# A two-layer GraphSAGE kernel on one core: nine dense groups instead of eight in layer 2, with h kept as two float32 parts for float32r products

## The chip, the core and the metric

The kernel runs on one core of one Trainium2 chip. The core has TensorE (PE) with its weight loads (PEld), VectorE (DVE), ScalarE (ACT), GpSimd (POOL) and the sync engine (SP), which here only issues transfers. The metric is the device time of one execution in microseconds, lower is better; of several executions the median is taken.

## The reference, cut to what matters

The inputs are x (12500 nodes x 256 features, float32), 200000 edges `src`, `dst` sorted by `dst`, and the weights of two layers and an output product. Low-numbered nodes have many more edges than high ones: `dst` is drawn as 12500 u^2.

```python
def _sage_conv(x, src, dst, W_l, b_l, W_r):
    msgs = x[src]
    agg = jax.ops.segment_sum(msgs, dst, num_segments=N_NODES)
    deg = jax.ops.segment_sum(jnp.ones((src.shape[0],), x.dtype), dst, num_segments=N_NODES)
    mean = agg / jnp.maximum(deg, 1.0)[:, None]
    return mean @ W_l + b_l + x @ W_r

h = relu(_sage_conv(x, src, dst, W1_l, b1, W1_r))
h = relu(_sage_conv(h, src, dst, W2_l, b2, W2_r))
out = layernorm(x + h @ W3 + b3)
```

## The kernel before

**Two ways to sum the edges.** Nodes are cut into 98 blocks of 128 (`NB = 98`), edges into 1563 tiles of 128. The destinations with the most edges are handled densely, in groups of 256 nodes (`DN = 256`). For such a group the kernel makes a table of counts (how often each of the 12544 source nodes points to each of the 256 destinations) in SBUF as bfloat16 and multiplies: the sums of the group are x^T times the counts, summed over all 98 source blocks. Layer 1 handles `HG1 = 6` groups (1536 nodes) in this way, layer 2 `HG = 8` groups (2048 nodes). All other edges are gathered: POOL issues one indirect transfer per tile (`L273`), which fetches 128 rows of 1 KB from x or h in DRAM. Four of them make a round. In a round four small products on PE (the strips, `part_ps`, L285) add up the rows of equal destination, ACT copies the result out (L295), a second product (`sum_ps`, L301) spreads it, and DVE adds it into a ring of sums (L315).

**Rounds set the order.** `layer` walks the rounds of gathers. Four buffers `got` hold the rows, so that POOL can be at most four rounds ahead of the strips on PE. PE and POOL run in the order in which the program is written; the other engines run their own queues in order too. After each round's strip the program places other work: pieces of the node blocks (the dense products with the weights), counting, and dense passes. How much goes into a round is set by a planner: each piece yields a cost for PE, DVE and ACT (`COST_1`, `COST_2` and so on), and a round is filled until the largest of the three loads reaches an allowance, 5.3 us in layer 1 and 5.2 us in layer 2. In the last rounds (8 in layer 1, 14 in layer 2) all that remains is placed.

**Layer 1's dense passes.** `count` makes the tables of the groups in the order 5, 4, 3, 2, 1, 0; two tables fit into SBUF (`both`), so each is used while the next one is made. `product` multiplies x with one table. Products of three bfloat16 parts of x give float32 accuracy; the parts lie in DRAM (`x3_d`) and are loaded for two blocks at a time (L747), six 256-column products per block (L750). As the parts do not exist at the start, the first pass and half of the second multiply float32 x with a widened float32 table (`wide`, L762, on ACT; L765 on PE), and these two passes make the parts on the side, one half of the blocks each (`parts`, L694 to L697: two DVE operations and two ACT copies per block). The tables of groups 5, 4, 3 and 2 are stored to DRAM for layer 2 (`stored`, seven transfers each).

**Layer 2's dense passes.** `first_block` writes h to DRAM, and its three bfloat16 parts to `h3_d`, again by `parts`. `products` takes two groups at a time: per block six products of 512 columns (L790), half of them into each of two PSUM tiles. Its rows are loaded for two blocks at a time (L717), four buffers deep. The first pass takes the tables of groups 1 and 0, which are still in SBUF; then come (5,4) and (3,2), whose tables are streamed from DRAM (L722) while the tables of 6 and 7 are counted, then (6,7) alone. Each finished group goes through `last_block`. A load of rows waits, by `freed`, for the strip that follows the last use of its buffer.

Of the kernel before, what the change touches and what calls it, by code (L numbers as in the profile page):

```python
# [8 lines left out]
F32 = mybir.dt.float32  # L9
# [16 lines left out]
P = 128  # L26
# [23 lines left out]
def by_runs(  # L50
# [55 lines left out]
    HG1, HG, DN = 6, 8, 256  # L106
# [6 lines left out]
    ROOMS = [5, 5, 7, 7] + [5] * 5 + [7] * 5 + [9] * 5 + [10] * 2  # L113
# [485 lines left out]
    SPLIT = 3  # L599
    split3 = keep.tile([P, SPLIT, 3, D], BF16, name="split")  # L600
# [10 lines left out]
    picks = [keep.tile([P, WIDEST * NB], BF16, name=f"pick{i}") for i in range(4)]  # L611
# [77 lines left out]
    def parts(t, s, rest):  # L689

        def upper(a):
# [8 lines left out]
    STREAMS = 4  # L700
    used_tables = tables[:, :sum(widths[:2 * HG1])]
    streams = [t.bitcast(BF16)[:, i * 4 * DN:(i + 1) * 4 * DN].rearrange("p (b g d) -> p b g d", b=2, g=2)
               for t in (spare, used_tables) for i in range(STREAMS // 2)]
# [9 lines left out]
    def loaded(b, pair):  # L713

        nonlocal n_streamed
        rows = rows_pool.tile([P, 2, 3, D], BF16, name="rows", bufs=N1)
        freed(nc.sync.dma_start(rows, h3_d[:, b:b + 2]), N1)  # L717
        counted = both[:, b:b + 2, :, :DN]
        if pair is not None:
            counted = streams[n_streamed % STREAMS]  # L720
            n_streamed += 1
            freed(nc.sync.dma_start(counted, count_d[:, b:b + 2, pair:pair + 2]), STREAMS)  # L722
        return rows, counted

    def product(g, c_sb, plain=range(0), made=range(0)):
# [4 lines left out]
        own, wide = {}, {}  # L730

        def x_rows(u):
            t = rows_pool.tile([P, 2, 3, D], BF16, name="rows", bufs=N1)
            t = t.rearrange("p b k d -> p (b k d)").bitcast(F32)[:, :2 * D].rearrange("p (b d) -> p b d", d=D)
            n = min(2, (N - u * P) // P)
            freed(nc.sync.dma_start(t[:, :n], x[u * P:(u + n) * P].rearrange("(b p) f -> p b f", p=P)), 1)
            if n < 2:
                left = N - (u + n) * P
                nc.vector.memset(t[:, n], 0.0)
                nc.sync.dma_start(t[:left, n], x[(u + n) * P:N])  # L740
            return t

        for b in range(NB):
            if b not in plain:
# [9 lines left out]
            else:  # L754
                if b % 2 == 0:
                    for u in range(b, min(b + 2 * N1 - 2, plain[-1]), 2):
                        if u not in own:
                            own[u] = x_rows(u)
# [749 lines left out]
```

## Time and profile before

| what | value |
|---|---|
| median of 3 runs | 2687.47 us (2685.69 to 2693.3) |
| profiled execution | 2681.34 us |
| its span | 2679.5 us |
| first to last gather of layer 1 | 11.4 to 1425.8 us, 1028 gathers |
| first to last gather of layer 2 | 1453.6 to 2637.0 us, 940 gathers |
| after the last gather | 42.5 us |
| granted clock of TensorE, mean | 0.968 |

The profile is of one execution. Busy times of PE overlap, since products are pipelined: the time that one product takes in a row of many is the distance from start to start, not its busy time. In the rows of a window a bracket like `(x940)` is the number of instructions. A wait is written as the engine and line that waits, then what ended the wait. Names of buffers have their numbers cut off, so `x_d` is `x3_d`, and `h_d` stands for both h and its parts.

### The profile page before, as it was taken

The numbers are of one execution on the slowest core, as the hardware profiler recorded it, in microseconds if no ns is written. First come the engines' busy times: TensorE is split into PE (matmuls) and PEld (weight loads), VectorE is DVE, ScalarE is ACT, GpSimd is POOL, SyncE is SP. The second block draws the span as 40 slices with busy tenths as digits, with TensorE's granted clock in tenths as the row PEclk, the third lists the DMA queues.
The fourth block names the chain that finished last, engine by engine and source line by source line (L and its number), as shares of the span: only waits on it lengthen the run. The fifth ranks groups of instructions, "written<-read, shape, count | busy, mean of one in ns | idle before, by whom it ended". The sixth has DMA issues, their size and how long they took to land. (4 is left out here: it accounts for less than half of the span.)

```text
span 2679.5 us, 51726 instructions
## 1 busy us (share of the span) xinstructions
PE 2411.8 (90%) x17119; PEld 1506.1 (56%) x17119; DVE 1558.3 (58%) x5514; ACT 1201.1 (45%) x2409; POOL 1910.2 (71%) x1978
## 2 busy tenths in 40 slices
PE   3678999889999999999997999999999999899986
PEld 2245676556776766666674445545455555555555
DVE  6777654775667789987334123544455554544455
ACT  0587764875667752386223012343434443222223
POOL 6767776776777777776664777777777777777772
PEclk8699999989999999999998999999999999999999
DMA  5359779889898777775875777778777777677653
GB/s 136 106 167 310 240 223 304 257 256 298 261 300 277 242 221 217 221 210 169 266 241 170 224 224 230 241 244 251 237 226 242 250 236 218 195 206 212 201 172 95
DMA packets 360737, 602.57 MB, mean 225 GB/s; under 512 B 56093, under 2 KB 244239, under 8 KB 360463
## 3 DMA queue, kind: packets, MB, share of 16 engines
q1 hardware_dynamic: 261637, 340.29, 39.8%
q0 software_dynamic: 94464, 258.08, 32.2%
q8 instruction: 141, 2.31, 0.4%
q10 hardware_dynamic: 4362, 0.80, 0.2%
q14 instruction: 133, 1.09, 0.1%
HBM read 509.09 MB, written 89.87 MB: 224 GB/s over the span
## 5 line engine op out<-in xcount | busy, mean ns | idle before, releaser
L273 POOL DMA_INDIRECT got<-in_x_dram,src_t x1028 | 1010.6, 983 | 412.3 <-issue 256.1
L273 POOL DMA_INDIRECT got<-h_d,src_t x940 | 897.3, 955 | 313.9 <-issue 251.4
L865 ACT CAST counts<-count_ps 128x882 f32 (+3 forms) x688 | 620.4, 902 | 232.7 <-PE count_ps L859 185.0
L859 PE MATMUL count_ps<-pick,low 128*128 128x490 bf16 (+2 forms) x1188 | 350.8, 350 | 56.9 <-ACT counts L865 44.9
L750 PE MATMUL dense_ps<-counts,rows 128*128 128x256 bf16 x2640 | 359.3, 276 | 23.3 <-DMA rows<-x_d 22.5
L285 PE MATMUL part_ps<-got,one 128*32 128x257 f32 (+1 forms) x3936 | 325.3, 403 | 58.7 <-DMA got<-h_d,src_t 34.8
L790 PEld LDWEIGHTS <-rows 128*128 128x128 bf16 x2352 | 214.0, 97 | 259.4 <-issue 81.4
L821 DVE TENSOR_SCALAR pick<-steps,tables 128x686 bf16<-128x686 f16 (+3 forms) x816 | 335.1, 411 | 24.7 <-PE count_ps L863 11.7
L295 ACT COPY some<-part_ps 128x257 f32<-128x257 f32 (+1 forms) x349 | 130.0, 373 | 472.5 <-PE part_ps L285 467.4
L750 PEld LDWEIGHTS <-rows 128*128 128x128 bf16 x2640 | 241.7, 98 | 104.8 <-issue 33.2
L229 DVE TENSOR_TENSOR one<-lo_t,lane_b 128x128 f32<-128x128 bf16 x492 | 140.7, 287 | 233.5 <-PE part_ps L285 232.3
L824 DVE TENSOR_SCALAR low<-lanes,low_t 128x130 bf16<-128x130 f16 x816 | 220.8, 272 | 82.5 <-PE count_ps L863 78.3
L315 DVE TENSOR_TENSOR sums<-sums,sum_ps 128x256 f32 x349 | 143.0, 410 | 154.6 <-PE sum_ps L301 134.8
L301 PE MATMUL sum_ps<-two,some 128*128 128x128 f32 x1396 | 222.6, 283 | 9.7 <-ACT own_t L997 7.6
L301 PEld LDWEIGHTS sum_ps<-two,some 128*128 128x128 f32 x1396 | 202.7, 195 | 41.4 <-ACT own_t L997 12.9
L790 PE MATMUL beside_ps<-counts,rows 128*128 128x512 bf16 x588 | 224.5, 382 | 0.5 <-ACT split L800 0.5
L790 PE MATMUL dense_ps<-counts,rows 128*128 128x512 bf16 x588 | 224.6, 382 | 0.0
L1038 DVE TENSOR_TENSOR own<-block_ps,biases 128x256 f32<-128x256 f32 x196 | 83.0, 424 | 216.9 <-PE block_ps L1031 214.5
L859 PEld LDWEIGHTS <-low 128*128 128x128 bf16 x1188 | 114.7, 99 | 150.4 <-issue 38.2
L285 PEld LDWEIGHTS part_ps<-got,one 128*32 128x32 f32 x3936 | 80.2, 109 | 202.5 <-issue 162.0
L997 ACT COPY own_t<-block_ps 128x256 f32<-128x256 f32 x294 | 105.4, 373 | 168.0 <-PE block_ps L995 164.8
L1034 ACT COPY sums<-zero 128x256 f32<-128x256 f32 x168 | 67.7, 403 | 240.9 <-PE block_ps L1031 240.9
(197 smaller groups left out, 3588.2 us busy)
## 6 DMA issues: line engine op xcount, KB each, us to landing
rows<-x_d SPq DMA_DIRECT2D x220, 384.0 KB
rows<-h_d SPq DMA_DIRECT2D x196, 384.0 KB
count_d<-counts SPq DMA_DIRECT2D x28, 896.0 KB
x_sb<-in_x_dram SPq DMA_DIRECT2D x194, 128.0 KB
h_d<-split SPq DMA_DIRECT2D x98, 192.0 KB
x_d<-split SPq DMA_DIRECT2D x98, 192.0 KB
rows<-in_x_dram SPq DMA_DIRECT2D x72, 256.0 KB
got<-in_x_dram,src_t POOLq DMA_INDIRECT x1028
```

The lines of the kernel that those rows point to most:

```text
L229: nc.vector.tensor_tensor(one, lo[:, a:a + n * (G - 1) + 1:n].unsqueeze(2).to_broadcast([P, G, W]), lane_b[:, :W].unsqueeze(1).to_broadcas ...
L273: rows = nc.gpsimd.indirect_dma_start(out=g[:, j, :D], out_offset=None, in_=self.table, in_offset=bass.IndirectOffsetOnAxis(ap=src_t[:, e: ...
L285: strip = nc.tensor.matmul(part_ps[j * W:(j + 1) * W, :width], lhsT=one[:, j], rhs=g[:, j, :width], start=r == 0, stop=r == n - 1)
L295: nc.scalar.copy(some[:, :width], part_ps[:, :width])
L301: nc.tensor.matmul(sum_ps[:, c], lhsT=some[:, c * P:(c + 1) * P], rhs=two, start=True, stop=True)
L315: adds.append(nc.vector.tensor_add(own, own, sum_ps[:, :NC]).ins)
L750: nc.tensor.matmul(ps[:, c], lhsT=rows[:, b % 2, k, c * P:(c + 1) * P], rhs=c_sb[:, b, :DN], start=False, stop=b == NB - 1 and k == 2 and ...
L790: nc.tensor.matmul(ps[c], lhsT=rows[:, b % 2, k, c * P:(c + 1) * P], rhs=counted[:, b % 2], start=b + k == 0, stop=b == NB - 1 and k == 2)
L821: nc.vector.tensor_scalar(r[:, :w * NB], steps[:, :w * NB], key_t[g][:, t - lo_g:t - lo_g + 1], None, op0=OP.is_equal)
L824: nc.vector.tensor_scalar(low.rearrange("p (a b) -> p a b", a=5), lanes_5[:, :, :LW // 5], low_t[:, t:t + 1], None, op0=OP.is_equal)
L859: nc.tensor.matmul(c[:, a * NB:b * NB], lhsT=s, rhs=r[:, a * NB:b * NB], start=True, stop=alone)
L865: nc.scalar.copy(to[:, :, bass.ds(off_act.at(t), w)], c.rearrange("p (d s) -> p s d", s=NB))
```

## The change

Layer 2:

- `HG` is 9: the destinations 2048 to 2303 become a dense group, and their edges are no longer gathered in layer 2.
- h is stored as two float32 parts (`exact`: the upper part by masking the low 12 bits of the float32, the lower as the difference), 2 KB per node instead of 1.5 KB. Both operations are on DVE; `parts` had two on DVE and two on ACT.
- The products take float32r operands. Per block and pair of groups there are four products of 512 columns instead of six. The bfloat16 tables must be widened to float32 first (`widened`, one ACT copy of 128x512 per block and pair).
- Rows are loaded per block (256 KB) into six buffers, issued four to five blocks ahead; tables are streamed per block into six buffers.
- The passes are (1,0), (5,4) while 6 and 7 are counted, (6,7), (3,2) while 8 is counted, and 8 alone. The last one has 256-column products, four per block, and one widening per two blocks.

Layer 1:

- No pass multiplies float32. The first pass makes the three bfloat16 parts of two blocks at a time (`parts_of`), writes them to `x3_d`, and multiplies them from the same buffer. All six passes have six 256-column bfloat16 products per block.

The allowances become 5.05 us in layer 1 and 5.04 us in layer 2. `pick` has three buffers instead of four, `split` two instead of three. `sums_a`, `sums_b` and `w3_sb` lie in parts of other tiles that are no longer needed.

```diff
-    HG1, HG, DN = 6, 8, 256
+    HG1, HG, DN = 6, 9, 256
-    h3_d = dram.tile([P, NB, 3, D], BF16, name="h3_d")
+    h2_d = dram.tile([P, NB, 2, D], F32, name="h2_d")
-    SAVED = ORDER[:HG1 - 2] + ORDER[HG1:HG - 2]
+    SAVED = ORDER[:HG1 - 2]
-    SPLIT = 3
-    split3 = keep.tile([P, SPLIT, 3, D], BF16, name="split")
+    split = keep.tile([P, 2, 2, D], F32, name="split")
-    picks = [keep.tile([P, WIDEST * NB], BF16, name=f"pick{i}") for i in range(4)]
+    picks = [keep.tile([P, WIDEST * NB], BF16, name=f"pick{i}") for i in range(3)]
+    def exact(t, s):
+        nc.vector.tensor_scalar(s[:, 0].bitcast(I32), t.bitcast(I32), -4096, None, op0=OP.bitwise_and)
+        nc.vector.tensor_tensor(s[:, 1], t, s[:, 0], op=OP.subtract)
-    STREAMS = 4
+    STREAMS = 6
+    N2, WIDE = 6, 4
-    def loaded(b, pair):
+    def loaded(b, of, back):
-        rows = rows_pool.tile([P, 2, 3, D], BF16, name="rows", bufs=N1)
-        freed(nc.sync.dma_start(rows, h3_d[:, b:b + 2]), N1)
+        rows = rows_pool.tile([P, 2, D], F32, name="rows", bufs=N2)
+        freed(nc.sync.dma_start(rows, h2_d[:, b]), back)
...
+    def widened(counted):
+        wide = rows_pool.tile([P, 2, DN], F32, name="wide", bufs=WIDE)
+        nc.scalar.copy(wide.bitcast(F32R), counted)
+        return wide
+    def parts_of(t, s):
+        rest = rows_pool.tile([P, 2, D], F32, name="rest_2", bufs=1)
+        nc.vector.tensor_tensor(rest, t, upper(t), op=OP.subtract)
+        freed(nc.vector.tensor_tensor(s[:, :, 2], rest, upper(rest), op=OP.subtract), N1)
+        freed(nc.scalar.copy(s[:, :, 0], upper(t)), N1)
+        nc.scalar.copy(s[:, :, 1], upper(rest))
...
-    def products(gs, pair):
+    def products(gs):
+        for b in range(0, NB, 2):
+            for u in range(b, min(b + 6, NB)):
+                if u not in held:
+                    held[u] = loaded(u, gs, b - (u - N2))
+            for u in range(b, min(b + 4, NB)):
+                if u not in wide:
+                    wide[u] = wide[u - 1] if one and u % 2 else widened(held[u][1])
...
+                            nc.tensor.matmul(ps[c], lhsT=own[:, k, c * P:(c + 1) * P].bitcast(F32R),
+                                             rhs=of.bitcast(F32R), start=u + k == 0,
+                                             stop=u == NB - 1 and k == 1)
...
-    COST_FIRST, COST_1, COST_2 = (0.92, 0.0, 0.31), (0.68, 0.0, 0.0), (0.7, 0.0, 0.0)
-    COST_DEGREES, COST_SPLIT, COST_REST = (0.4, 0.0, 0.0), (0.0, 0.71, 0.81), (0.0, 0.0, 0.3)
+    COST_ONE = 1.1, 0.0, 0.65
+    COST_FIRST, COST_1, COST_2 = (0.68, 0.61, 0.7), (0.68, 0.0, 0.0), (2.0, 0.0, 1.24)
+    COST_DEGREES, COST_REST = (0.4, 0.0, 0.0), (0.0, 0.0, 0.3)
...
+        yield [passed(*ORDER[4:6])]
+        yield [passed(*SAVED[0:2]), (next_counts(ORDER[6:8]), counting(*ORDER[6:8]))]
+        yield [passed(*ORDER[6:8])]
+        yield [passed(*SAVED[2:4]), (next_counts(ORDER[8:]), counting(*ORDER[8:]))]
+        yield [passed(*ORDER[8:])]
...
-        layer(gathers_1, first_block, 3, staged(stages_1), 5.3, 8)
+        layer(gathers_1, first_block, 3, staged(stages_1), 5.05, 8)
...
-    layer(Gathers(h_d, True), last_block, 5, staged(stages_2), 5.2, 14)
+    layer(Gathers(h_d, True), last_block, 5, staged(stages_2), 5.04, 14)
```

`COST_2` was the cost of three products and is now that of two blocks, which have eight; `COST_ONE` and `COST_FIRST` are for two blocks of the pass of group 8 and for one block of layer 1's first pass.

More of the change, by code (lines that the diff above doesn't have):

```diff
@@ L1075, in first_block @@
         nc.sync.dma_start(h_d[b * P:(b + 1) * P, :], h)
[L1076 to L1079 removed]
+        s = split[:, b % 2]
+        exact(h, s)
+        nc.sync.dma_start(h2_d[:, b], s)
+        yield 1.75, 1.65, 1.1
     def last_block(b, agg=None):
```

160 lines of the change are left out of this document (67 added, 93 removed).

## The prediction

> **What bounds the kernel now.** First the page's head and a table of stretches: up to the last gather of layer 1, between the layers, layer 2's gathers, the end.
>
> ```profile
> span 2679.5 us, 51726 instructions
> ...
> core 0: us, PE busy (x) PEld busy (x) DVE busy (x) ACT busy (x) POOL busy (x), PEclk, DMA share, GB/s
> 11.40:1425.80 1414.40, 1264.25 (x10145) 857.88 (x10145) 983.15 (x3664) 816.81 (x1571) 1010.62 (x1028) 0.95 0.75 235
> 1425.80:1453.60 27.80, 16.24 (x86) 11.21 (x84) 14.83 (x49) 11.15 (x32) 0.01 (x1) 0.91 0.52 171
> 1453.60:2637.00 1183.40, 1103.90 (x6752) 616.72 (x6752) 530.57 (x1690) 360.78 (x772) 897.29 (x940) 0.99 0.72 221
> 2637.00:2679.50 42.50, 25.32 (x132) 18.57 (x130) 21.88 (x64) 12.39 (x35) 0.02 (x1) 0.94 0.20 57
> ```
>
> With the 11.4 us before the first gather: 11.4 + 1414.4 + 27.8 + 1183.4 + 42.5 = 2679.5. PE is the engine with the largest busy time, but that is modelled and overlaps; the question is what paces the rounds. Two neighbouring gathers, and the gathers by form:
>
> ```profile
> 2603.32 0.95 POOL L273 DMA_INDIRECT got<-h_d,src_t  x1 [0.30 <-issue]
> 2604.57 0.95 POOL L273 DMA_INDIRECT got<-h_d,src_t  x1 [0.30 <-issue]
> ```
> ```profile
> L273 POOL DMA_INDIRECT got<-in_x_dram,src_t x1028 | 1010.6, 983 | 412.3 <-issue 256.1 <-PE part_ps L285 119.0 <-DMA got<-in_x_dram,src_t 10.9
> L273 POOL DMA_INDIRECT got<-h_d,src_t x940 | 897.3, 955 | 313.9 <-issue 251.4 <-DMA h_d<-split 27.8 <-DMA got<-h_d,src_t 12.2
> ```
>
> A gather comes every 1.25 us when POOL waits for nothing: 0.95 busy, 0.30 between. Four make a round, so 5.0 us is the floor of a round. Layer 2 takes 1183.4/940 = 1.259 us for each, 8 us above its floor of 1175 in all; no wait for PE is in its row. **Layer 2 is paced by POOL.** Layer 1 takes 1414.4, 129 above its floor of 1028 x 1.25 = 1285, and its row names PE's strips (119.0 us): PE reaches them late, since other work stands before them in its order. Where, by gathers per stretch (40 per 50 us is the floor's rate):
>
> ```profile
> 0.00:250.00 250.00, 174.71 (x169) 0.86 0.59 174
> 250.00:1425.80 1175.80, 835.90 (x859) 0.97 0.79 247
> 400.00:450.00 50.00, 29.84 (x31) 0.90 0.93 309
> 750.00:800.00 50.00, 36.06 (x38) 0.93 0.94 300
> 1250.00:1400.00 150.00, 98.43 (x105) 0.98 0.79 255
> ```
> ```profile
> PEld L750 <- DMA rows<-x_d: 30.1, 26, 3.4
> ```
>
> Columns are POOL busy, gathers, PE clock, DMA share and GB/s. After 250 us, 859 gathers need 1175.8, 102 above 859 x 1.25 = 1074. The low ones are 400 to 450, where tables are stored while parts of x are loaded, and 1250 to 1400, where dense passes run with no counting beside them. PE also waits for rows of x3 there, 30 us in all.
>
> **Layer 1, part by part.** Prices of PE are distances from start to start:
>
> ```profile
> 1306.24 1.48 PE L750 MATMUL dense_ps<-counts,rows 128*128 128x256 bf16 x12
> 1307.56 0.61 PE L301 MATMUL sum_ps<-two,some 128*128 128x128 f32 x4
> ...
> 1654.64 0.38 PE L790 MATMUL dense_ps<-spare,rows 128*128 128x512 bf16 x1
> ...
> 1655.51 0.61 PE L301 MATMUL sum_ps<-two,some 128*128 128x128 f32 x4
> 1655.95 0.37 PE L859 MATMUL count_ps<-pick,low 128*128 128x490 bf16 x1
> ...
> 1656.37 0.38 PE L790 MATMUL dense_ps<-spare,rows 128*128 128x512 bf16 x1
> ...
> 1657.11 0.64 PE L285 MATMUL part_ps<-got,one 128*32 128x256 f32 x8
> 1657.68 0.39 PE L790 MATMUL beside_ps<-spare,rows 128*128 128x512 bf16 x1
> ...
> 1658.98 1.03 PE L1024 MATMUL block_ps<-w2l_sb,sums 128*128 128x256 f32 x4
> 1659.85 1.03 PE L1031 MATMUL block_ps<-w2r_sb,own_t 128*128 128x256 f32 x4
> ```
>
> So a 256-column bfloat16 product costs 1.32/12 = 0.110; a 512-column one 0.87/4 = 0.217 (four from 1654.64); a spread 0.44, so 0.11 for each of its four records, and 0.22 for turning a block, which is two such records; counting one tile 0.42; a strip 0.57; a float32 product of 256 columns, which leaves two records, 0.87/2 = 0.43.
>
> - PE: 148 blocks of float32 go (98 in the first pass, 50 in the second): 296 x 0.43 = 127 us. They come back as bfloat16: 888 x 0.110 = 98. Net -29.
> - ACT and DVE, by these rows:
>
> ```profile
> L865 ACT CAST counts<-count_ps 128x980 f32 x36 | 37.6, 1045 | 21.1 <-PE count_ps L859 19.8 <-ACT own_t L997 0.4
> L762 ACT CAST wide<-counts 128x512 f32<-128x512 bf16 x74 | 45.6, 618 | 0.2 <-PE dense_ps L765 0.2
> L697 ACT COPY split<-rest 128x256 bf16<-128x256 bf16 x196 | 78.4, 405 | 4.2 <-DVE rest L694 2.6
> L695 DVE TENSOR_TENSOR split<-rest 128x256 bf16<-128x256 f32 x196 | 80.6, 416 | 38.0 <-DMA x_d<-split 33.9 <-DMA h_d<-split 3.4
> ```
>
> ACT loses 74 widenings (46 us) and 392 copies of parts (392 x 0.405 = 159), and gains 98 copies of 128x512, which no row has: between 0.405 and the widening's 0.618, nearest to the latter by size, 61. Net -144 (-165 to -144). DVE loses 392 operations of 0.416 (163), gains 196 for h of the same size (82) and 98 of double width, between 0.416 and 0.83, taken at 0.72 (71). Net -10 (-40 to 0). POOL keeps its 1028 gathers. On SP, 98 writes of x3 become 49, loads of x 74 become 49, loads of x3 220 become 245, and h's parts grow from 192 to 256 KB; the bytes are nearly the same, so the stretch at 400 stays crowded.
>
> None of these engines sets the floor, so the sums are not gained directly. What is gained is time in which PE reaches a strip late. The allowance falls from 5.3 to 5.05 us per round, with less work to place. After 250 us there are 859/4 = 215 rounds at 5.47; 0.25 us less in each is 54 us, half of the 102 above the floor. I take -54. Ends: 0, if the late strips come from stored tables and late rows, which stay; and -102. The first 250 us, with setup and counting without a dense pass, keep their time, with `pick` one buffer shorter; nothing for that. Layer 1: 1360.4. The gap of 27.8 and the tail of 42.5 stay: the last blocks have the same products; two ACT copies fewer in each block of layer 1, at most 1 or 2 us, go against a larger rest placed in its last eight rounds.
>
> **Layer 2, part by part.** The program of the changed kernel has 908 gathers of h, 32 fewer: eight rounds, 32 x 1.259 = 40.3 us straight off the path, if POOL remains what paces. So every other resource has to fit into 5.04 us per round.
>
> Weight loads of the dense products, bfloat16 and float32:
>
> ```profile
> L790 PEld LDWEIGHTS <-rows 128*128 128x128 bf16 x2352 | 214.0, 97 | 259.4 <-issue 81.4 <-DMA h_sb<-h_d 0.8 <-DMA tables<-count_d 0.8
> L765 PEld LDWEIGHTS dense_ps<-wide,rows 128*128 128x128 f32 x592 | 105.8, 193 | 28.4 <-ACT wide L762 8.8 <-issue 7.4 <-ACT split L696 0.8
> ```
>
> - PE now: dense 2352 x 0.217 = 510; strips 235 x 0.57 = 134; spreads 169 x 0.44 = 74; blocks 98 x (3 x 0.87 + 2 x 0.22) = 299; counts of 6 and 7, 136 tiles x 0.42 = 57. Sum 1074, 4.57 per round. After: 564 for the rest, -6 for eight strips and four spreads, 56 tiles of group 8 at 0.47 (wider by a ninth) +26, group 8's 392 products of 256 columns at 0.13 (between 0.110 and a weight load's 0.193 of the second row, nearer to the former, since loads overlap) +51: 635, and 1568 float32r products of 512 columns. No row shows float32r. Its bounds are bfloat16's 0.217 and, at twice the columns of L1024, float32's 0.87. I take 0.217: the code cuts h into parts of 12 bits, which is needed only if a product takes fewer bits than float32 and so fewer passes, and the planner books 2.0 us for eight, 0.25 each, which is a booking and not a measurement. Then 635 + 340 = 975, 4.3 per round: PE falls away further as a bound.
>
> The Trainium skill, "FP8 and Floating Point Precision", section "TensorE Precision Notes", says that true FP32 takes four passes and that reduced-precision FP32 reads four bytes and truncates them to FP22; by that, one pass and my value. The trace agrees for the first half (0.43 against 0.110), and cannot show the second. Against the change speaks the Trainium skill's "TensorE: Matmul & The Clock Gate", section "Weight-path perf modes — Fast Weight Load (FWL) and DoubleRow": the fast weight load is not used for FP32. The trace agrees, with 193 ns for float32 loads against 97.
>
> - Weight loads: in float32 products they lie beside the product before (0.217 from start to start with loads of 193 ns), so 512 columns hide them.
>
> PE's wait for the widening between 240 and 400 us, and the issue of a load of rows:
>
> ```profile
> PE dense_ps L765 <- ACT wide L762: 4.7, 4, 2.0
> ```
> ```profile
> L717 SPq DMA_DIRECT2D rows<-h_d x196: 319/320/1359, 1423.7 to 2559.1; - x196
> ```
>
> - ACT gains 441 widenings x 0.618 = 273 and 56 counts of 1.05 (59): 361 + 332 = 693 of some 1150 us, 60%. They stand in order with the copies of the strips, and PE now waits for them. In layer 1's float32 passes PE waited for them little (4.7 us between 240 and 400). A widening that waits for its table or for a free buffer holds up what is behind it on ACT: copies of strips and counts, and through them PE's spreads. It is issued two to four blocks before its use, so I take 5 us for all of it.
> - Transfers: h's rows become 490 x 256 KiB = 128.5 MB instead of 196 x 384 KiB = 77.1; tables 25.7 as before; gathers -4.2. From 221 GB/s x 1183.4 = 261.5 MB to 308.7, over 1160 us 266 GB/s, and the share from 0.72 to 0.87. In the passes without counting ((1,0), (6,7), 8: about 87 rounds by the program's order) three to four blocks go into a round, some 300 GB/s, with six buffers of one block: one and a half to two rounds of lead, where there were nearly three. On SP a load that waits for its buffer holds up the loads of h and x for the blocks and the writes of the output behind it, as now; SP issues 686 loads for the passes instead of 294, at 0.32 us each some 0.6 us more per round, which fits. The row at 750 had 300 GB/s and 38 gathers in 50 us, 5.26 per round, with other causes in it. I take 0.14 over 87 rounds, 12 us; ends 0 and, as in 1250 to 1400 (150/105 x 4 = 5.71), 0.68 x 87 = 59.
>
> Layer 2: 1183.4 - 40.3 + 5 + 12 = 1160.1. **Sum:** 11.4 + 1360.4 + 27.8 + 1160.1 + 42.5 = 2602.2 of span. The profiled execution was 1.8 above its span and the median of the runs 6.1 above that execution, so 2610 us as a median, -2.9%. A change of under 0.3%, 8 us, can't be told from none.
>
> **The rivals.**
> 1. Both layers reach their floors: -48 more in layer 1, -17 in layer 2, 2545. For it: everything gets lighter. Against it: stored tables crowd the queue as before. Chance 0.08.
> 2. Layer 1 gives nothing back: 2664. For it: the wait for rows at 400 and 1250 to 1400 and a queue as full as before. Chance 0.12.
> 3. Rows of h come late: 59 instead of 12 in layer 2, 2657. PE waiting for rows puts strips late, and POOL waits for PE, as now only in layer 1. Chance 0.12. Together with 2, 2711, slower: 0.07.
> 4. On the other side: float32r costs more. Layer 2 may last 1160 + 77 = 1237 before all is lost; (1237 - 635)/1568 = 0.38 us per product is where it turns. If a product left two passes, 0.43, PE needs 635 + 674 = 1309, 5.8 per round: 2759. The same comes if the weight load isn't hidden: 0.217 + 0.193 = 0.41. For it: no float32r in the trace. Against it: loads of that size hidden in all float32 products. Chance 0.10.
>
> My forecast has 0.51. Faster: 0.51 + 0.08 + 0.12 + 0.12 = 0.83, less 0.03 into no change for the upper edges of 2 and 3: 0.80; the same 0.04; slower 0.16. The range from 2555 to 2685 holds the forecast, 2, 3 and the edge of 1, and leaves out 4 and both together; the forecast's own is 2580 to 2640.
>
> **What would show it.** Right: gathers of h every 1.25 to 1.28 us, 908 of them, with hardly a wait for PE; float32r products 0.22 apart; the wait of x's gathers for part_ps down from 119 to some 65; DMA share in layer 2 0.85 to 0.9. Wrong: float32r records in pairs or 0.4 apart; PE waiting for rows of h or for `wide` by tens of us; ACT's strip copies late behind widenings; gathers longer than 0.95 from full queues.

## The result, and the profile after

The changed kernel takes 2727.2 us as a median of 4 runs (2713.2 to 2732.5), the kernel before 2686.6 in the same series: 1.0139 of it, 95% interval 1.0096 to 1.0182. Forecast were 2610; the sign was wrong, and the time lies above the range. The profiled execution took 2732.5 us. Its head, and the same four stretches as in the prediction (up to the last gather of layer 1, between the layers, layer 2's gathers, the end):

```profile
span 2730.5 us, 52904 instructions
...
PE 2353.6 (86%) x17114; PEld 1628.3 (60%) x17114; DVE 1578.7 (58%) x5575; ACT 1406.1 (51%) x2533; POOL 1895.6 (69%) x1946
```
```profile
26.00:1396.90 1370.90, 1228.38 (x10439) 836.21 (x10440) 969.57 (x3572) 715.96 (x1215) 1019.98 (x1027) 0.95 0.78 248
1396.90:1427.90 31.00, 18.46 (x91) 12.84 (x89) 14.35 (x49) 7.59 (x22) 1.00 (x3) 0.84 0.57 184
1427.90:2690.00 1262.10, 1082.37 (x6493) 762.35 (x6493) 573.20 (x1864) 673.14 (x1273) 872.38 (x908) 0.97 0.77 245
2690.00:2730.50 40.50, 22.43 (x86) 15.32 (x86) 14.20 (x41) 8.12 (x23) 0.00 (x0) 0.73 0.11 33
```

These windows are cut a few us beside the first and last gathers. From the first and the last gather of each layer itself the span adds up as follows (us):

| | before first gather | layer 1's gathers | between | layer 2's gathers | after last | span |
|---|---|---|---|---|---|---|
| before | 11.4 | 1414.4 | 27.8 | 1183.4 | 42.5 | 2679.5 |
| forecast | 11.4 | 1360.4 | 27.8 | 1160.1 | 42.5 | 2602.2 |
| after | 29.6 | 1368.5 | 29.7 | 1256.7 | 46.0 | 2730.5 |

Layer 1 gave nearly what was forecast. Two things went the other way: the start lost 18 us, and layer 2, with 32 gathers fewer, takes 73 us more. The gathers by form:

```profile
L273 POOL DMA_INDIRECT got<-in_x_dram,src_t x1028 | 1021.0, 993 | 374.4 <-issue 262.8 <-PE part_ps L285 44.4 <-DVE src_t L404 26.8
L273 POOL DMA_INDIRECT got<-h_d,src_t x908 | 872.4, 961 | 414.0 <-issue 253.5 <-PE part_ps L285 136.3 <-DMA got<-h_d,src_t 7.9
```

The wait for PE's strips (`part_ps`) fell from 119.0 to 44.4 us in layer 1 and came up in layer 2, from nothing in the row to 136.3. Where in layer 2, by POOL's busy time, gathers, PE clock, DMA share and GB/s (40 gathers in 50 us are the floor's rate):

```profile
1450.00:1500.00 50.00, 37.81 (x41) 1.00 0.94 315
1500.00:1550.00 50.00, 37.81 (x41) 1.00 0.92 300
1650.00:1700.00 50.00, 31.58 (x33) 1.00 0.68 211
1700.00:1750.00 50.00, 27.41 (x28) 0.93 0.62 195
1850.00:1900.00 50.00, 28.22 (x30) 0.92 0.63 193
2050.00:2100.00 50.00, 37.80 (x41) 1.00 0.91 299
```

It isn't where rows of h are loaded fastest: pass (1,0), up to 1590, and (6,7), at 2050, keep the floor's rate at 300 GB/s and a share above 0.9. It is the stretch from 1590 to 1950, pass (5,4) with the counting of groups 6 and 7, and transfers are lowest there. PE's and POOL's main waits in it (total, times, longest), and its engines' busy time:

```profile
POOL got L273 <- PE part_ps L285: 93.2, 46, 5.7
PE count_ps L886 <- ACT counts L892: 74.8, 76, 1.5
...
1590.00:1950.00 360.00, 277.19 (x1597) 182.80 (x1598) 185.65 (x653) 223.39 (x340) 213.59 (x220) 0.95 0.65 200
```

In the kernel before, while the same tiles were counted (1640 to 2240), PE had no wait for the copy of a count, and POOL waited little:

```profile
ACT counts L865 <- PE count_ps L859: 98.6, 99, 2.8
...
POOL got L273 <- PE part_ps L285: 4.0, 13, 0.3
```

What the wait is, from the timeline of PE and ACT of the changed kernel:

```profile
1689.64 0.39 PE L820 MATMUL beside_ps<-wide,rows 128*128 128x512 f32 x1
...
1691.02 0.39 PE L820 MATMUL beside_ps<-wide,rows 128*128 128x512 f32 x1
1691.25 0.61 PE L301 MATMUL sum_ps<-two,some 128*128 128x128 f32 x4
...
1692.37 1.00 ACT L892 CAST counts<-count_ps 128x882 f32 x1 [0.30 <-PE count_ps L886]
1693.41 0.37 PE L886 MATMUL count_ps<-pick,low 128*128 128x490 bf16 x1 [0.57 <-ACT counts L892]
...
1694.08 1.00 ACT L892 CAST counts<-count_ps 128x882 f32 x1 [0.47 <-PE count_ps L886]
1695.13 0.37 PE L886 MATMUL count_ps<-pick,low 128*128 128x490 bf16 x1 [1.14 <-ACT counts L892]
1695.80 1.04 ACT L892 CAST counts<-count_ps 128x882 f32 x1 [0.72 <-PE count_ps L886]
```

Layer 2 has one PSUM buffer for counts (`count_ps`). Where two tiles stand next to one another in PE's order, the second can't start before ACT has copied the first out: 1693.41 to 1695.13, 1.72 us, in which PE works for 0.6. What stands behind it on PE, strips among it, waits with it. Layer 1 of the same run has two such buffers and shows the other case. From its timeline:

```profile
134.22 4.15 ACT L892 CAST counts<-count_ps 128x882 f32 x4
...
136.30 0.37 PE L886 MATMUL count_ps<-pick,low 128*128 128x490 bf16 x1 [0.45 <-ACT counts L892]
...
137.36 0.37 PE L886 MATMUL count_ps<-pick,low 128*128 128x490 bf16 x1 [0.48 <-ACT counts L892]
```

Here the copies run without a break, and neighbouring tiles of 882 columns lie 1.04 us apart (median of 41 pairs), about the length of the copy, against 1.72 (38 pairs, none under 1.67) in layer 2. **The theory** after this reading: the chain PE, copy, PE costs layer 2 its time, because the tiles of 6 and 7 now stand beside one pass, in large pieces. From the first copy of their counts to the last it is 592 us in the kernel before (1650.4 to 2242.1) and 371 now (1576.3 to 1947.6). A pass yields to the planner after three products in the kernel before (392 pieces over two passes, 136 tiles) and after eight in the changed one (49 pieces, 136 tiles), so that several tiles must follow each other between two pieces. In the kernel before no two of the 136 tiles are neighbours on PE. In the changed one, between 1590 and 1950, 49 pairs of 130 tiles are, in the median 1.74 us apart. That is 49 x (1.74 - 0.42) = 65 us more of PE's time than tiles that stand alone would take, an estimate, and the stretch lost 85: its 220 gathers need 275 of the 360 us.

**The rivals:** ACT has too much to do (the widenings), float32r products are slow, or rows of h are late. The last falls by the table of stretches. The products lie 1.61/7 = 0.23 us apart within a piece (1689.64 to 1691.25, seven products), one record each, with weight loads of 0.195 us beside them.

The start is a matter of its own. DVE's order has the first operation of `parts_of`, which waits for x, ahead of the tables of source numbers that the first gather needs:

```profile
27.33 0.69 DVE L747 TENSOR_TENSOR rest<-x_pair 128x512 f32<-128x512 f32 x1 [16.94 <-DMA x_pair<-in_x_dram]
28.67 1.55 DVE L404 TENSOR_SCALAR src_t<-src_ps 128x512 int32<-128x512 f32 x3
...
29.64 1.63 POOL L273 DMA_INDIRECT got<-in_x_dram,src_t  x1 [26.76 <-DVE src_t L404]
```

### The profile page after: what moved, and what is told of

The parts are those of the page before. It is cut to its first block, busy times and chain, and to the rows that moved or that the text cites. A ratio compares the mean times of both kernels' runs of the same rounds, so it can differ in the third digit from the quotient of the medians.

```text
span 2730.5 us, 52904 instructions
## 1 busy us (share of the span) xinstructions
PE 2353.6 (86%) x17114; PEld 1628.3 (60%) x17114; DVE 1578.7 (58%) x5575; ACT 1406.1 (51%) x2533; POOL 1895.6 (69%) x1946
## 5 line engine op out<-in xcount | busy, mean ns | idle before, releaser
L892 ACT CAST counts<-count_ps 128x882 f32 (+3 forms) x744 | 681.5, 916 | 254.0 <-PE count_ps L886 196.7
L785 PE MATMUL dense_ps<-counts,rows 128*128 128x256 bf16 x3528 | 486.7, 277 | 27.1 <-DMA rows<-x_d 22.6
L886 PE MATMUL count_ps<-pick,low 128*128 128x490 bf16 (+2 forms) x1300 | 386.4, 352 | 137.5 <-ACT counts L892 125.6
L785 PEld LDWEIGHTS <-rows 128*128 128x128 bf16 x3528 | 324.5, 98 | 139.4 <-issue 45.7
L848 DVE TENSOR_SCALAR pick<-steps,tables 128x686 bf16<-128x686 f16 (+3 forms) x872 | 361.4, 417 | 23.0 <-PE count_ps L886 12.8
L820 PE MATMUL dense_ps<-wide,rows 128*128 128x512 f32 x784 | 340.7, 435 | 2.0 <-DMA rows<-h_d 1.6
L820 PE MATMUL beside_ps<-wide,rows 128*128 128x512 f32 x784 | 316.1, 403 | 0.0
L301 PE MATMUL sum_ps<-two,some 128*128 128x128 f32 x1380 | 224.6, 287 | 19.4 <-ACT own_t L1012 13.1
L737 ACT CAST wide<-counts 128x512 fp32r<-128x512 bf16 x245 | 151.2, 619 | 143.2 <-PE beside_ps L820 110.1
L856 DVE TENSOR_SCALAR aft<-steps,tables 128x98 bf16<-128x98 f16 x745 | 187.4, 252 | 0.0
L820 PEld LDWEIGHTS dense_ps<-wide,rows 128*128 128x128 f32 x784 | 153.2, 195 | 57.0 <-issue 23.4
```

What stands on the lines that cost most here:

```text
L301: nc.tensor.matmul(sum_ps[:, c], lhsT=some[:, c * P:(c + 1) * P], rhs=two, start=True, stop=True)
L737: nc.scalar.copy(wide.bitcast(F32R), counted)
L785: nc.tensor.matmul(ps[:, c], lhsT=rows[:, b % 2, k, c * P:(c + 1) * P], rhs=c_sb[:, b, :DN], start=False, stop=b == NB - 1 and k == 2 and ...
L820: nc.tensor.matmul(ps[c], lhsT=own[:, k, c * P:(c + 1) * P].bitcast(F32R), rhs=of.bitcast(F32R), start=u + k == 0, stop=u == NB - 1 and k ...
L848: nc.vector.tensor_scalar(r[:, :w * NB], steps[:, :w * NB], key_t[g][:, t - lo_g:t - lo_g + 1], None, op0=OP.is_equal)
L856: nc.vector.tensor_scalar(aft.rearrange("p (a b) -> p a b", a=7), steps_7[:, :, :NB // 7], after_t[g][:, t - after_from[g]:t - after_from[ ...
```

## The experiments

Results are medians and ratios to the kernel before, run on the same chip. "Layer 2" is the time from its first to its last gather, of one profiled execution. It varies from one execution to the next: the first experiment, whose edit leaves layer 2 as it is, has 1243.9, which is 12.8 below the changed kernel's. A difference of that size can't be told from none.

**The start.** `later` is the helper by which the program puts an instruction behind what its engine has first.

```diff
-        nc.vector.tensor_tensor(rest, t, upper(t), op=OP.subtract)
+        later(nc.vector.tensor_tensor(rest, t, upper(t), op=OP.subtract))
```

> The changed kernel, but the first subtraction of each pair in parts_of may only start once the tables for the first gathers are there. Theory of the start: DVE, which runs in order, had that subtraction ahead of the tables for the first gathers and waited 16.9 us for x, so the first gather came at 29.6 us instead of 11.4. Then the first gather comes at about 11.5 us and the whole is about 16 to 18 us shorter (2709). Rival: the parts of x only move, and layer 1 takes back what it gains: under 6 us.

2709.7 us, 1.0101 (1.0058 to 1.0144). The first gather is back at 11.6 us, as expected; of the 18.0 at the start, layer 1's gathers gave 9.4 back (1377.9). The median is 17.5 below the changed kernel's, but the two intervals overlap. So the delay of the first gather and its cause are shown; what it costs the whole is not measured as well. It is 18 of the 128 us by which the span missed its forecast.

**Widenings on DVE,** to take 441 copies off ACT.

```diff
-        nc.scalar.copy(wide.bitcast(F32R), counted)
+        nc.vector.tensor_copy(wide.bitcast(F32R), counted)
```

> The changed kernel with the 441 widenings on DVE instead of ACT, in the same order on PE. Theory of ACT's load: counts are copied late because widenings stand in ACT's queue; then the slow stretch of layer 2 (30 gathers per 50 us between 1600 and 1950) goes back to 38 or more, 60 us or more shorter. Theory of the chain: each tile of counts goes PE, ACT, PE through the only bank for counts, 1.72 us from tile to tile when three stand next to each other, whatever else is on ACT; then PE still waits some 60 to 75 us for ACT's copies of counts, and the whole is at most 25 us shorter.

2719.6 us, 1.0114 (1.0077 to 1.0151), layer 2 1249.5. The same stretch:

```profile
POOL got L273 <- PE part_ps L285: 78.7, 43, 4.1
PE count_ps L886 <- ACT counts L892: 71.2, 73, 1.5
...
1590.00:1950.00 360.00, 277.67 (x1654) 183.02 (x1655) 230.34 (x759) 175.24 (x258) 224.04 (x232) 0.98 0.68 210
```

ACT has 48 us less to do there (223 to 175), and PE waits for its copies as before (74.8 to 71.2). Layer 2's 7 us lie within the spread. ACT's load isn't the cause.

**Eight groups with float32r,** counting beside two passes as in the kernel before.

```diff
-    HG1, HG, DN = 6, 9, 256
+    HG1, HG, DN = 6, 8, 256
...
-        yield [passed(*SAVED[0:2]), (next_counts(ORDER[6:8]), counting(*ORDER[6:8]))]
+        two = [passed(*SAVED[0:2]), passed(*SAVED[2:4])]
+        yield [(chain.from_iterable([p for p, _ in two]), sum(whole for _, whole in two)),
+               (next_counts(ORDER[6:8]), counting(*ORDER[6:8]))]
         yield [passed(*ORDER[6:8])]
-        yield [passed(*SAVED[2:4]), (next_counts(ORDER[8:]), counting(*ORDER[8:]))]
-        yield [passed(*ORDER[8:])]
```

> The changed kernel with eight dense groups in layer 2: 940 gathers of h, and the counts of 6 and 7 stand beside two passes, (5,4) and (3,2), as in the kernel before; float32r and widenings stay. Theory of the chain: with 1.7 tiles of counts in a round instead of 2.7 the chain is hidden; layer 2's gathers take about 1190 us (5.06 per round) in spite of 32 more, the whole about 2660. Theory of ACT's load: widenings per block are the same, so the counting stretch stays above 5.5 per round, layer 2 above 1240, the whole 2715 or more. If eight groups lose 40 us of gathers and gain nothing, 2770.

2676.4 us, 0.9961 (0.9932 to 0.9990): 51 less than with nine groups, though 32 gathers more. Layer 2 takes 1211.1, 21 above the chain theory's expectation and 29 below what the load theory had as its least. 26 pairs of tiles are still neighbours, for the pieces are as large as in the changed kernel, and PE's wait for copies in the counting is half as long (1580 to 2080):

```profile
PE count_ps L886 <- ACT counts L892: 37.6, 38, 1.5
POOL got L273 <- PE part_ps L285: 30.2, 24, 5.7
```

**Nine groups, 6 and 7 counted beside two passes.** Then 8 has no pass left to be counted beside.

```diff
+        two = [passed(*SAVED[0:2]), passed(*SAVED[2:4])]
+        yield [(chain.from_iterable([p for p, _ in two]), sum(whole for _, whole in two)),
+               (next_counts(ORDER[6:8]), counting(*ORDER[6:8]))]
...
-        yield [passed(*SAVED[2:4]), (next_counts(ORDER[8:]), counting(*ORDER[8:]))]
+        yield [(next_counts(ORDER[8:]), counting(*ORDER[8:]))]
```

> The changed kernel, nine groups, but the counts of 6 and 7 stand beside two passes, (5,4) and (3,2); then (6,7), then the counts of 8 with no pass beside them, then 8. Same work in another order. Theory of the chain: the long slow stretch goes (-80), a short one comes where 8 is counted, 56 tiles at 3 or more per round, 15 to 18 rounds at 6 us or more (+20); layer 2's gathers about 1195 us instead of 1257, the whole about 2670. Theory of ACT's load: no change beyond 15 us.

2723.1 us, 1.0132 (1.0082 to 1.0183), layer 2 1247.0: no gain to speak of, and my expectation missed. The slow stretch had moved: between 1590 and 1950 the wait for copies is 22.9 instead of 74.8, but where 8 is counted alone and shortly after (2330 to 2520) there are 114 gathers in 190 us, and

```profile
POOL got L273 <- PE part_ps L285: 53.1, 23, 5.7
PE count_ps L886 <- ACT counts L892: 37.1, 37, 1.6
```

The last count is copied at 2473.3 and the first widening comes at 2474.3, so the counting is slow here without a single widening on ACT. Up to 2474 it loses 43 us above the floor, where 20 were expected; the pass of 8 behind it loses 31 more, and the expectation had nothing for that. What makes that pass slow isn't shown.

**Rotated passes:** (1,0), then (5,4) beside the counting of 6, (3,6) beside 7, (2,7) beside 8, and 8; with the start mended. A pass of one stored and one fresh table widens them in two ACT copies.

```diff
-        yield [passed(*SAVED[0:2]), (next_counts(ORDER[6:8]), counting(*ORDER[6:8]))]
-        yield [passed(*ORDER[6:8])]
-        yield [passed(*SAVED[2:4]), (next_counts(ORDER[8:]), counting(*ORDER[8:]))]
+        yield [passed(*SAVED[0:2]), (next_counts(ORDER[6:7]), counting(*ORDER[6:7]))]
+        yield [passed(SAVED[2], ORDER[6]), (next_counts(ORDER[7:8]), counting(*ORDER[7:8]))]
+        yield [passed(SAVED[3], ORDER[7]), (next_counts(ORDER[8:]), counting(*ORDER[8:]))]
```

> Nine groups with the counts spread over three passes: (1,0), then (5,4) beside the counts of 6, (3,6) beside those of 7, (2,7) beside those of 8, and 8 alone; the start as in e1_start. A pass with one streamed and one resident table widens in two ACT copies per block. Theory of the chain: with 1.5 to 1.7 tiles of counts per round everywhere, PE waits little for ACT's copies; layer 2's gathers take 1160 to 1185 us, the whole 2615 to 2640, faster than both kernels. If float32r passes are slow for a reason of their own (rows, widening), layer 2 stays above 1215 and the whole above 2670.

2642.4 us, 0.9840 (0.9804 to 0.9877), below both kernels. Layer 2 takes 1179.1, as expected: 77.6 less than in the changed kernel with the same groups and products, and 64.8 less than in the one with the start alone mended. 20 pairs of 192 tiles are neighbours; the waits in all of layer 2, which were 136.3 and 88.4:

```profile
POOL got L273 <- PE part_ps L285: 46.9, 50, 3.8
PE count_ps L893 <- ACT counts L899: 35.5, 36, 2.8
```

**Layer 1 alone:** layer 2, h and its three parts as in the kernel before, layer 1's passes and allowance as in the changed one, start mended.

```diff
-    HG1, HG, DN = 6, 9, 256
+    HG1, HG, DN = 6, 8, 256
-    h2_d = dram.tile([P, NB, 2, D], F32, name="h2_d")
+    h3_d = dram.tile([P, NB, 3, D], BF16, name="h3_d")
...
-    layer(Gathers(h_d, True), last_block, 5, staged(stages_2), 5.04, 14)
+    layer(Gathers(h_d, True), last_block, 5, staged(stages_2), 5.2, 14)
```

> The kernel before with layer 1's passes of the changed one (bfloat16 parts made in the first pass, allowance 5.05, three buffers for pick) and the start as in e1_start; layer 2 and h's three bfloat16 parts as before. The trace of the changed kernel has layer 1's gathers in 1368 us instead of 1414; so 2640 to 2650 if that gain is the passes' own, since here ACT still makes the parts of h in layer 1. If it came from h's two parts being made on DVE alone, 2675 or more.

2650.4 us, 0.9878 (0.9853 to 0.9904), at the upper edge of the first expectation. Layer 1's gathers take 1385.1, 29.3 less than before, and layer 2's 1183.2, as before. So layer 1's gain is its own. Set beside the eight groups in float32r (layer 2 1211.1), the same 940 gathers take 28 us less with bfloat16 parts; but the two also differ in the size of the pieces and in the allowance (5.04 and 5.2).

**A shorter copy, by leaving work out:** in layer 2 only the first five columns of a tile of counts are copied out; the other counts are left out of the tables, so the sums of groups 6 to 8 are incomplete.

```diff
-                nc.scalar.copy(to[:, :, bass.ds(off_act.at(t), w)], c.rearrange("p (d s) -> p s d", s=NB))
+                e = 5 if g >= HG1 else w
+                nc.scalar.copy(to[:, :, bass.ds(off_act.at(t), e)], c[:, :e * NB].rearrange("p (d s) -> p s d", s=NB))
```

> The changed kernel with only the first five of nine or ten columns of each tile of counts copied out in layer 2; the rest of the table is left out, so its counts are incomplete. ACT's copy in the chain falls from 1.02 to some 0.76 us. Theory of the chain: from tile to tile 1.45 instead of 1.72 us, the slow stretch (80 us above the floor) loses 30 to 50, the whole about 2690. Rival, that the stretch is slow through PE's own work or through rows: under 10 us.

2687.6 us, 1.0015 (0.9998 to 1.0031), 39 below the changed kernel; layer 2 1214.7, 42 less. The copy of 490 columns takes 753 ns where 882 took 1016, neighbours lie 1.49 us apart (median) instead of 1.74, and 1590 to 1950 has

```profile
POOL got L273 <- PE part_ps L285: 52.4, 43, 2.8
PE count_ps L886 <- ACT counts L893: 48.6, 68, 1.1
```

All of PE's work is still there, and over the whole of layer 2 its wait for copies falls from 88.4 to 58.0 us and POOL's wait for strips from 136.3 to 93.3, as much as layer 2 itself. The whole is at the 2690 that the theory of the chain gave.

**The allowance of the rotated kernel in layer 2,** 4.92 instead of 5.04:

> As e5_rotate with layer 2's allowance at 4.92 instead of 5.04 us: the work is spread further towards the end. If what is left above the floor in e5_rotate is rounds that are filled too full, some 10 us less; if the rest that is placed after the last gathers grows by more than it saves, the same or longer.

2671.8 us, 0.9950 (0.9931 to 0.9968), 29 above the rotated kernel: what isn't placed in the rounds is left for the last 14, where POOL waits once for 41.3 us (at 2572.1; the 14 rounds begin at 2510.6):

```profile
POOL got L273 <- PE part_ps L285: 72.3, 40, 41.3
```

**The copy split over two engines,** all work kept: 56 of 98 blocks by ACT, 42 by DVE, in the changed kernel and in the rotated one; and the rotated one with 5.2.

```diff
-                nc.scalar.copy(to[:, :, bass.ds(off_act.at(t), w)], c.rearrange("p (d s) -> p s d", s=NB))
+                of = c.rearrange("p (d s) -> p s d", s=NB)
+                n = 56 if g >= HG1 else NB
+                nc.scalar.copy(to[:, :n, bass.ds(off_act.at(t), w)], of[:, :n])
+                if n < NB:
+                    nc.vector.tensor_copy(to[:, n:, bass.ds(off_dve.at(t), w)], of[:, n:])
```

> The changed kernel with all its work; in layer 2 each tile of counts is copied out by two engines at once, 56 of the 98 blocks by ScalarE and 42 by VectorE. Chain theory (each tile goes PE, copy, PE through a single PSUM buffer, 1.72 us from tile to tile): the copy falls from 1.02 to some 0.75 us (a half copy took 0.753), so 1.45 from tile to tile; PE's waits for ACT's and DVE's copies of counts between 1590 and 1950 fall from 74.8 to 35 to 55 us; layer 2's gathers take 1220 to 1240 instead of 1257; 2690 to 2712 in time. Load theory (the engines have too much to do, not the order of three steps): the two copies together are more work than the one, so the waits stay and the time is 2720 to 2745.

> The rotated passes (each group's counting beside a pass of its own, start mended) with the copy of each tile of counts split over ScalarE and VectorE as well. Chain theory: what is left of PE's waits for copies of counts in layer 2, 35.5 us, falls to 15 to 25, layer 2's gathers from 1179 to 1160 to 1172, time 2615 to 2635. If the rest of layer 2's loss has other causes (blocks' own chains, late rows): no change, 2638 to 2650.

> The rotated passes with layer 2's allowance at 5.2 us per round instead of 5.04. If work left for the last rounds is what costs (at 4.92 it was 29 us slower, with one wait of 41 us near the end): layer 2's gathers take 1165 to 1176, time 2625 to 2640. If full rounds cost more than the end (PE reaches strips late all along): 1185 to 1200, time 2648 to 2665.

These fell on a chip where the kernel before takes 3188.9 us, some 19% longer, as did a second series on another chip (3190.9) and a third on one more (3144.3). Only ratios within a series can be used. In the order of the expectations the first series gave 1.0307 (1.0269 to 1.0344), 1.0089 (1.0059 to 1.0119) and 1.0068 (1.0040 to 1.0096); the second, of the same three, much the same: 1.0355 (1.0314 to 1.0395), 1.0113 (1.0075 to 1.0152) and 1.0068 (1.0039 to 1.0097). All lie above the ranges of the chain theory, which were for chips like the first.

> The changed kernel with the copy of each tile of counts in layer 2 split over ScalarE (56 blocks) and VectorE (42), taken on a chip like that of the other runs. Chain theory: from tile to tile about 1.45 us instead of 1.72, PE's waits for copies of counts between 1590 and 1950 at 35 to 55 us instead of 74.8, layer 2's gathers 1220 to 1240 us, time 2690 to 2712, ratio to before 1.002 to 1.010. Load theory: 2720 to 2745.

> The rotated passes with the split copy. Chain theory: layer 2's gathers 1160 to 1172 us instead of 1179, time 2615 to 2635, ratio to before 0.974 to 0.982. If the rest has other causes: 2638 to 2650.

> The rotated passes with an allowance of 5.2 instead of 5.04 in layer 2. If the work left for the last rounds costs: 2625 to 2640. If full rounds cost more: 2648 to 2665.

As the changed kernel itself was missing beside them, the third series had it, its split copy, the rotated kernel and that with the split copy:

> The changed kernel as it is, so that the split copy and the rotated passes have it beside them on the same chip. On a chip like that of the first runs: 1.010 to 1.018 of before. On one where every kernel takes 19% longer the ratio is open: if PE is what is held up there, the changed kernel with its longer chains of PE loses more, 1.02 to 1.04.

> The changed kernel with the copy of counts split over two engines. Chain theory: 0.985 to 0.995 of the changed kernel's time on the same chip, from tile to tile 1.45 us instead of 1.72. Load theory: 0.997 to 1.007 of it.

> The rotated passes, beside the changed kernel on the same chip: 0.965 to 0.975 of its time if the chain of counts and the start are the cause there too.

> The rotated passes with the split copy. Chain theory: 0.990 to 0.997 of the rotated kernel's time on the same chip. Other causes for what is left: 0.998 to 1.003.

| third series | median, us | to the kernel before | layer 2 |
|---|---|---|---|
| changed | 3221.2 | 1.0234 (1.0202 to 1.0265) | 1462.1 |
| changed, split copy | 3249.9 | 1.0343 (1.0307 to 1.0379) | 1484.4 |
| rotated | 3190.4 | 1.0114 (1.0050 to 1.0178) | 1450.1 |
| rotated, split copy | 3205.0 | 1.0184 (1.0143 to 1.0226) | 1465.7 |

The split made the changed kernel slower, 1.009 of its time, where the chain theory had 0.985 to 0.995. For the rotated kernel it is 1.005, where 0.990 to 0.997 was expected; there the intervals overlap, so only the missing gain is shown. The trace of the changed kernel with the split copy tells why:

```profile
2005.52 0.64 ACT L894 CAST counts<-count_ps 128x504 f32 x1 [0.30 <-PE count_ps L886]
2006.19 0.55 DVE L896 CAST counts<-count_ps 128x378 f32 x1
2006.80 0.37 PE L886 MATMUL count_ps<-pick,low 128*128 128x490 bf16 x1 [0.80 <-DVE counts L896]
...
2007.47 0.64 ACT L894 CAST counts<-count_ps 128x504 f32 x1 [0.94 <-PE count_ps L890]
2008.14 0.55 DVE L896 CAST counts<-count_ps 128x378 f32 x1
2008.74 0.37 PE L886 MATMUL count_ps<-pick,low 128*128 128x490 bf16 x1 [1.36 <-DVE counts L896]
```

The two copies don't run at once: in each of the 192 tiles DVE starts 0.03 us or more after ACT has ended. Both read the same buffer. The chain has a step more and got longer, 1.94 us here, 2.08 in the median of 51 pairs against 1.74 in the changed kernel of this series. So the edit did the opposite of what it was made for, and the time went the way of the chain: 51 x 0.34 = 17 us for the neighbours, and layer 2 takes 22 more, a size that must be read with the spread above in mind. In the counting (1880 to 2300) ACT's busy time falls from 243 to 181 us meanwhile. The Trainium skill, "PSUM — Partial Sum Buffer", section "PSUM bank collisions raise a hardware error", says that no two of the engines may access the same bank within the same partition at the same time, two readers included, and that the compiler back end's scheduler adds a dependency between two such instructions. The order seen here agrees; what put the two copies in this order isn't shown. Each half of the split by blocks has all nine or ten columns of a tile, and so both parts of the buffer into which PE writes columns 0 to 4 and the rest; a split by columns wasn't tried.

The rotated kernel takes 0.990 of the changed one's time on that chip, where 0.965 to 0.975 was expected: 31 us and not 85 as on the first chips, and 12 of them in layer 2. It isn't faster than the kernel before there. So on that chip the chain isn't shown to be what costs layer 2 its time. The 5.2 us of allowance has no rotated kernel with 5.04 in its series and decides nothing.

## Why the prediction was wrong

**The step that failed** is the cost of counting. The prediction put it as "counts of 6 and 7, 136 tiles x 0.42 = 57" of PE, and 56 tiles of group 8 at 0.47, with the copies as a sum of ACT's busy time (59 us). Both durations are right; neither is what a tile costs where the next one follows it. There it is PE, copy and PE in series, 1.74 us. The kernel before never paid it: no two tiles were neighbours, because 392 small pieces of two passes lay between 136 tiles. The change took half the passes from beside them and made the pieces eight products long, and the prediction, which read the list of passes as an order of work only, didn't ask how many tiles now stand between two pieces. None of the rivals had this form: rival 4 named the point from which layer 2 loses everything, 1237 us, and layer 2 passed it (1256.7) with float32r at 0.26 us instead of the 0.38 that would have been needed.

Layer 2 point by point, from 1183.4:

- 32 gathers fewer, -40.3: as said, 908, which leaves 1143. What came on top is 1256.7 - 1143.1 = 113.6, against 17 forecast.
- It is lost where tiles are counted. The floor is 1.25 us for each gather. What layer 2 takes above it (us), up to the first tile of counts, from there to the last one, and behind that (one gather more or less at an edge makes 1.25):

| kernel | up to the counting | counting | behind it | sum |
|---|---|---|---|---|
| before | -1.1 | 7.5 | 2.0 | 8 |
| changed | -0.4 | 106.2 | 15.8 | 122 |
| rotated | -0.3 | 27.8 | 16.7 | 44 |
| eight groups, float32r | -0.4 | 29.8 | 6.8 | 36 |

- Of the 106, 85 lie between 1590 and 1950, 5 in (6,7), and 15 where 8 is counted beside (3,2). The forecast had 25 above the floor in all.
- 65 to 78 of the 113.6 go when the counting is rotated, without a change of groups or products (1179.1). That the chain does it is shown by the shorter copy, which takes 42 us off layer 2 with PE's work as it was, and by the widenings on DVE, which take more off ACT and change little. The longer copy adds 22 on the slower chip, the way that the chain has it.
- The other 36 stay with the rotated passes. By the table some 20 of what the rotated kernel has above the kernel before lie in the counting, where PE's waits for copies (35.5 us) are left, and 15 in the pass of 8. What makes that last pass slow isn't settled: in the rotated kernel PE waits there 3.9 us for rows and its weight loads 9.9, and PE 24 for the blocks' own steps on DVE and ACT.
- **Float32r at 0.217:** 0.23 within a piece, one record, loads hidden: right as a price of one. A piece's first product after other work costs more (0.31 at 1689.33), and over the 1384 pairs of neighbouring products in layer 2 the distance is 0.26 in the mean, where the bfloat16 products before have 0.22. That is 1568 x 0.043 = 67 us more on PE than the sum had, 0.3 per round; it doesn't make PE the bound, but the room that was thought to be there was smaller. The pass (1,0), with float32r and widenings at every block, loses nothing above the floor, so these aren't slow of themselves. Yet eight groups in bfloat16 are the faster ones: of the 28 us some 22 lie in the counting, where the large pieces leave 26 pairs of neighbours. Bfloat16 in pieces as large was not run.
- **Widenings, +5 on ACT:** moving them off ACT gives 7 us in layer 2, which is within the spread. Nothing speaks against the size.
- **Late rows, +12 in the passes without counting:** (1,0) and (6,7) kept 40 or 41 gathers per 50 us at up to 315 GB/s. The third, the pass of 8, lost 15.8 us; PE waits in it 7.2 us for rows and its weight loads 13.1, so the 12 may lie there. Rival 3, with 59, falls.

Layer 1: -54 forecast, -45.9 measured, and the wait for strips fell to 44.4 where "some 65" was forecast; with the start mended it is 54.9 to 65.4. That fits the mechanism that was forecast. But "the first 250 us ... keep their time" was wrong by 18.2: the moved `parts_of` was followed on PE, ACT and the queues and not on DVE, whose first operation now waits for x. With the start mended layer 1's gathers take 1378 to 1385, -29 to -37, so a part of the -45.9 was the late start given back, and the term of -54 was too large. The gap and the tail kept their size within 4 us.

## What to carry to other kernels

A step that goes through one buffer and two engines has two prices: its busy time, if enough other work lies between two of them, and the whole way there and back, if not. When a change takes cover away or makes its pieces larger, count how many such steps now stand between two pieces of other work; a planner that books loads by engine doesn't see it. The Trainium skill, "Perfetto Trace Analysis", section "Matmuls", says that independent groups of products should go round several PSUM banks, so that one is emptied while the next is filled; the 1.72 us between neighbouring tiles through one buffer in layer 2, against 1.04 through two in layer 1, agree. A second buffer in layer 2 wasn't tried. And follow a moved operation on every engine that it issues to: DVE, which keeps to its order, stood 16.9 us before one subtraction that waited for a transfer, and the tables behind it came as late.

## What the runs showed of the hardware

On three chips the kernel before took 17 to 19% longer than on those of the other runs, the changed one 18% and the rotated one 21%, so the differences between kernels weren't the same. On POOL, ACT and DVE single instructions take as long as elsewhere: in the changed kernel a gather of h 956 ns against 961, a copy of 882 columns 1015 against 1016. On PE they are a few per cent longer (the products of counts 397 ns against 381), and the mean granted clock is 0.91 against 0.957. What is longer most of all is the idle time, on several engines at once. It isn't the clock alone: from 700 to 800 us the rotated kernel has a granted clock of 1.00 there and issues 67 gathers, against 75 at 0.97 in its first run. In the rotated kernel of the third series:

```profile
737.10 0.59 DVE L855 TENSOR_SCALAR pick<-steps,tables 128x686 bf16<-128x686 f16 x1 [1.75 <-PE count_ps L893]
737.16 0.92 ACT L899 CAST counts<-count_ps 128x686 f32 x1 [1.69 <-PE count_ps L893]
...
738.12 0.37 PE L893 MATMUL count_ps<-pick,low 128*128 128x490 bf16 x1 [1.61 <-issue]
738.13 0.10 PEld L897 LDWEIGHTS <-low 128*128 128x128 bf16 x1 [1.79 <-issue]
```

DVE and ACT stand for 1.7 us and go on within 0.06 us of one another, though the product that is named last ended at 735.9; then PE stands for 1.6 without a wait that the profile shows. What holds them up isn't in the traces and stays open. A tuned order of work was worth 3% on one chip here and 1% on another (2642.4 against 2727.2, and 3190.4 against 3221.2).
